# Column sums of a masked spectral kernel moved by two units and into the tail's norm, two gathers issued earlier, and a ring of 15 tiles instead of 13

## The chip, the cores and the metric

The kernel runs on one core of a Trainium2 chip. The core has five instruction streams: TensorE (PE, with its weight loads listed as PEld), VectorE (DVE), ScalarE (ACT), GpSimd (POOL) and SyncE (SP, here used to issue DMAs). Every stream takes its instructions in the order in which the program gives them and waits on semaphores for the others. Sixteen DMA engines move data between the device memory and the on-chip memory. The metric is the time of one execution in microseconds (us); lower is better.

## What is computed

The input `x` is one image of 512 x 512 positions with 64 channels (67 MB in float32). Two layers are applied, each to a group-normalised copy of its input, and each added to its input:

```python
x = x + _L0_conv_ref(_gn(x), mask, ...)   # masked triangle product with gates
x = x + _L1_conv_ref(_gn(x), w_real, w_imag)

# layer 0: xn = ln(x); left, right = masked, gated projections of xn
out = jnp.einsum('bkjd,bkid->bijd', left, right)
out = (_ln(out) @ out_w + out_b) * sigmoid(xn @ ogate_w + ogate_b)

# layer 1: the lowest 12 x 12 modes of a 2-D Fourier transform, mixed over channels
x_ft = jnp.fft.fft2(xc, axes=(-2, -1))[:, :, :12, :12]
out_ft = jnp.einsum('bcmn,comn->bomn', x_ft, w)
out = real(ifft2(out_ft padded with zeros))
```

The second layer needs three things of the first layer's whole result `x1`: the mean and variance of each of 32 groups of channels, the 12 x 12 modes, and `x1` itself, to which the inverse transform is added.

## The kernel before

The kernel looks at the mask on the chip. If at most 256 rows are kept by it, which is so here, it takes the path `compact`, where rows of the image are sorted so that the kept ones come first. The first stages (to about 812 us) make the triangle product, which lies in `places`, a buffer of 8 places of 4096 floats per partition, and put its layer-normed, projected result in `u_d` in device memory.

**The unit loop.** `x1` is then made in 32 units. A unit is a pair of 32 image columns (`jc`, 16 of them) and a half of the rows (`half`, two blocks of 128 rows). A unit `v` has 8 steps `n`; `s` counts steps over all, `k = v + 8`. `last` is unit 31. Each step's work is written down by hand in the order in which the engines shall take it: PE transposes data 13 steps ahead (`transpose`), multiplies for the gate of this step (`times`, tile `w_ps`) and for the centred values 12 steps ahead (`c_ps`); every fourth step it adds into the row transform (`transform`). DVE multiplies by the inverse deviation (L1144), adds a bias, sums squares and makes the statistics of the second norm from the unit before (L1051). ACT evacuates, squares and takes the sigmoid. POOL multiplies the gate in (`gated`, L1002) and adds into `x1` (`added`, L1006), and issues the gathers that load later units (`load`, L628). SP issues all stores of `x1` (`store`, into `x1_h[0]` for the left 256 image columns, `x1_h[1]` for the right), the 32 row loads of `u_d` for every second unit (`load_u`), and the writes of the row transform (`save`, into `modes_d`). In units `v % 4 == 1` the statistics of four units are joined (`join_means`, `join_squares`, `join_rest`).

**The column sums.** The column part of the transform is taken in four pieces of 128 image columns, `h` = 0 to 3. `fetch(h)` loads a piece of `modes_d` into `modes_t` (place 7, first part), and `columns(h, pool)` has PE do 12 small matmuls on it (24 passes in the trace, L888) into a PSUM tile of the transposes' pool `t_ps`, which has two slots, and DVE add them to `sums` (L889). In the loop the load is issued on SP in step 6 of units 8, 16 and 24 (L1167) and the sums come in step 6 of units 9, 17 and 25 (L1169):

```python
if n == 6 and v % 8 == 0 and 0 < v < len(units):
    fetch(v // 8 - 1)
if n == 6 and v % 8 == 1 and 8 < v < len(units):
    columns(v // 8 - 1, ps_t)
```

In unit 30, SP issues the load of the mixing weights `wide` into places 3 to 5 (L1173; float positions 12288 to 21504).

**The tail.** POOL clears `picks`, the mixing's operand (L1192), loads the fourth piece of modes (`fetch(3)`, on POOL), then issues `AHEAD` = 13 gathers, each of one tile of `x1` (128 rows x 32 image columns x 64 channels, 1,048,576 bytes) from `x1_h` into a ring of buffers: one behind `wide` in `places` (positions 21504 to 23552), halves of the places 6, 2, 0, 1 and 7, and three extra tiles `lx_t`. Meanwhile DVE and PE finish the second norm (`group_norm_affine`: a reduction, the matmul `mean_ps`, five DVE operations, the matmul `var_ps`, the inverse root), then do `columns(3)`, the product `turned`, the filling of `picks`, 288 small matmuls that mix the channels (`mixed_ps`, L1224), and the inverse transform over columns (`back_columns`). After that 64 tiles are finished one by one: four matmuls (`l_ps`, L1286), four additions on DVE (L1293), a store by SP (L1294), and a gather of the tile that is 13 further on into the same buffer (L1298 to L1300). Three more `back_columns` come between.

Of the kernel before, what the change touches and what calls it, by code (L numbers as in the profile page):

```python
# [17 lines left out]
P = 128  # L18
# [13 lines left out]
K = 2 * P  # L32
AHEAD = 13
SHARE = 22
# [12 lines left out]
def conv_preact_kernel(ctx: ExitStack, tc: tile.TileContext, t: dict):  # L47
# [135 lines left out]
    def rsqrt(pool, total, scale, eps, shape, y=None):  # L183

        out, steps = rsqrt_steps(pool, total, scale, eps, shape, y)
        for step in steps:
            step()
        return out  # L190
# [49 lines left out]

    def group_norm_affine(keep, sets, each, name):

# [4 lines left out]
        with tc.tile_pool(name="gn_" + name, bufs=1) as gp, tc.tile_pool(  # L247
# [4 lines left out]
            mean_ps = gps.tile([P, groups], F32, name="mean_ps")  # L252
            nc.tensor.matmul(mean_ps, avg, part, start=True, stop=True)
            mean = gp.tile([P, groups], F32, name="mean")
            nc.vector.tensor_scalar(mean, mean_ps, 1.0 / (n * each), None, ALU.mult)
# [8 lines left out]
            var_ps = gps.tile([P, groups], F32, name="var_ps")  # L264
            nc.tensor.matmul(var_ps, avg, v, start=True, stop=True)
            rs = rsqrt(gp, var_ps, 1.0 / n, EPS, [P, groups])
            if groups == G:
# [344 lines left out]
    def compact(fc):  # L612
# [193 lines left out]
        with tc.tile_pool(name="tri", bufs=1) as trp:  # L806
# [57 lines left out]
            with tc.manual_schedule(), tc.tile_pool(name="late", bufs=1) as lp:  # L864
# [17 lines left out]

                def columns(h, pool):
                    by = modes_t.rearrange("p (m k) c -> p m (k c)", k=2)
                    ps = pool.tile([P, 4, P], F32, name="t_ps").rearrange("p i k -> p (i k)")[:, : MODES * M2]
                    ps = ps.rearrange("p (m n) -> p m n", m=MODES)
                    for m in range(MODES):
                        nc.tensor.matmul(ps[:, m, :], by[:, m, :], col_basis[:, h, :], start=True, stop=True)  # L888
                    nc.vector.tensor_add(sums, sums, ps)  # L889

                def fetch(h):

                    (nc.gpsimd if h == 3 else nc.sync).dma_start(modes_t, modes_d[h * P : (h + 1) * P])

                with tc.tile_pool(name="np_x", bufs=LEAD + 2) as tp, tc.tile_pool(
# [179 lines left out]
                    for s in range(-LEAD, total_g + 2 * SIZE):  # L1075
# [44 lines left out]
                        if 0 <= v + 3 < len(units):  # L1120
                            if n == 3:
                                load(v + 3, 0)
                            if n == 6:
                                load(v + 3, 1)

                        if n >= 3 and held(1):
# [40 lines left out]
                        if n == 6 and v % 8 == 0 and 0 < v < len(units):  # L1167
                            fetch(v // 8 - 1)
                        if n == 6 and v % 8 == 1 and 8 < v < len(units):  # L1169
                            columns(v // 8 - 1, ps_t)  # L1170
# [4 lines left out]
                with tc.tile_pool(name="lq", bufs=1) as qp, tc.tile_pool(name="lx", bufs=1) as xp:  # L1175

                    free = 3 * 64 * C + C * MODES * MODES
                    buffers = [places[:, free : free + JC * C].rearrange("p (n c) -> p n c", c=C)]
                    buffers += [place(i)[:, r * JC : (r + 1) * JC] for i in (6, 2, 0, 1) for r in range(2)]
                    buffers += [place(7)[:, JC:]]  # L1180
                    buffers += [xp.tile([P, JC, C], F32, name=f"lx_t{i}") for i in range(AHEAD - len(buffers))]
                    ranked = [h.rearrange("s (k j) c -> (s k) (j c)", k=NJ // 2) for h in x1_h]
                    tiles_left = [(jc, b) for jc in range(NJ) for b in range(4)]
                    xts = {}

                    def fetch_rows(jc, b):
                        xts[jc, b] = buffers[(4 * jc + b) % AHEAD]
                        gather(xts[jc, b].rearrange("p j c -> p (j c)"), ranked[jc // 8], dst_i, b, jc % 8)


                    picks = qp.tile([P, MODES, MODES, 32], F32, name="picks")
                    nc.gpsimd.memset(picks, 0.0)  # L1192
                    fetch(3)
                    for jb in tiles_left[:AHEAD]:
                        fetch_rows(*jb)
                    rinv = qp.tile([P, 4, P], F32, name="rinv")
                    nc.scalar.dma_start(rinv, t["c_rinv"])
                    col_inv = qp.tile([P, 2, 4, P], F32, name="col_inv")
                    nc.scalar.dma_start(col_inv, t["c_col_inv"])
                    ab2 = group_norm_affine(lp, sets, 8, "x1c")  # L1200
                    with tc.tile_pool(name="tcp", bufs=1, space=PSUM) as tcp:
                        columns(3, tcp)
                    with tc.tile_pool(name="sps", bufs=1, space=PSUM) as sps:
# [16 lines left out]
                        for m3 in range(3):  # L1220
                            for n in range(MODES):
                                for g in range(4):
# [3 lines left out]
                                        start=(n == 0), stop=(n == MODES - 1), tile_position=(0, 32 * g),  # L1226
                                    )

                        mixed = qp.tile([P, 3, C], F32, name="mixed")
# [45 lines left out]
                    with tc.tile_pool(name="lpq", bufs=1, space=PSUM) as pq, tc.tile_pool(  # L1275
                        name="lpt", bufs=2, space=PSUM
                    ) as pt, tc.tile_pool(name="lps", bufs=4, space=PSUM) as pp:
                        for jc in range(NJ):
                            for b in range(4):
                                it = parts[:, jc // 8, (jc % 8) * N : (jc % 8 + 1) * N]  # L1280
                                xt = xts.pop((jc, b))
                                group = []
# [16 lines left out]
                                if ahead < len(tiles_left):  # L1299
                                    fetch_rows(*tiles_left[ahead])  # L1300
                                if jc % 4 == 1 and b == 0 and jc // 4 < 3:
# [72 lines left out]
```

## Time and profile before

| what | us |
|---|---|
| median of three runs (1876.83 to 1881.99) | 1879.58 |
| the profiled execution, its own time | 1877.87 |
| its span, first to last instruction | 1876.0 |
| unit loop, units 0 to 31 (812 to 1534.8) | 723 |
| end of the loop to the first finished tiles (1534.8 to 1580) | 45 |
| tiles of the second layer (1580 to 1876) | 296 |

The page gives, over the span, PE 88% busy, DVE 78%, ACT 51%, POOL 47%, and 250 GB/s moved by DMA on average. A span's mean hides that the stages differ, so the shares are to be read by stage: PE is busy for 674 of the 723 us of the unit loop, DVE for 675; the DMA engines are busy for 0.98 of the last 296 us. A line of the timeline reads: start, duration, engine, line of the program, operation, result and operands, count, and in brackets how long the engine had been idle before it and what ended that.

### The profile page before, as it was taken

Reading aid. Unit: us, or ns where it says so; the run is one execution under the profiler, and the core shown is the slowest. Engines: PE = TensorE matmul, PEld = TensorE weight load, DVE = VectorE, ACT = ScalarE, POOL = GpSimd, SP = SyncE. Lnnn points to the kernel's source line nnn. Section 1 sums busy time; section 2 is a strip of 40 time slices with the busy share of each in tenths; the row PEclk is TensorE's granted clock in tenths of the full one; section 3 lists DMA queues with packets and bytes.
Section 4 is the critical chain, followed back from the end, with each engine's and each line's share of the span. In section 5 each row is a group of like instructions: output and inputs, shape, how many; then the busy total and the mean of one; then the engine's idle time right before and its main releaser. Section 6 shows DMA issues by size and latency. Waiting matters only on the chain. (4 is left out here: it accounts for less than half of the span.)

```text
span 1876.0 us, 33850 instructions
## 1 busy us (share of the span) xinstructions
PE 1653.0 (88%) x11598; PEld 1302.6 (69%) x11598; DVE 1454.2 (78%) x3001; ACT 953.8 (51%) x1670; POOL 873.8 (47%) x678
## 2 busy tenths in 40 slices
PE   6779899999899999899998999899989957997873
PEld 5666666664787777788887988788879835664441
DVE  5989677777455559989998899899989994664552
ACT  3665466554222278777776677677757720111000
POOL 3655111111000000059999799989979982111110
PEclk9989899999899999999999999999989976555555
DMA  6999155556655534347876677767666599999999
GB/s 251 390 380 377 59 135 139 140 138 160 206 180 175 168 127 180 136 151 263 267 258 231 226 252 252 266 222 241 235 240 229 189 252 365 414 426 427 426 427 382
DMA packets 188869, 468.23 MB, mean 250 GB/s; under 512 B 35184, under 2 KB 134384, under 8 KB 147600
## 3 DMA queue, kind: packets, MB, share of 16 engines
q1 hardware_dynamic: 158192, 262.40, 41.3%
q0 software_dynamic: 27856, 202.19, 28.0%
q8 instruction: 94, 1.54, 0.3%
q10 hardware_dynamic: 2640, 1.38, 0.3%
q14 instruction: 87, 0.71, 0.1%
HBM read 278.13 MB, written 187.76 MB: 248 GB/s over the span
## 5 line engine op out<-in xcount | busy, mean ns | idle before, releaser
L943 PE MATMUL w_ps<-gate_x,xt_c 128*128 128x128 f32 x2048 | 283.3, 283 | 30.2 <-DVE z_t L1144 28.8
L1006 POOL TENSOR_TENSOR places<-places,z_t 128x1024 f32<-128x1024 f32 x127 | 301.8, 2377 | 8.2
L943 PEld LDWEIGHTS w_ps<-gate_x,xt_c 128*128 128x128 f32 x2048 | 254.4, 195 | 47.5 <-DVE z_t L1144 45.7
L943 PE MATMUL c_ps<-center_x,xt_c 128*128 128x128 f32 x2048 | 277.7, 279 | 6.1 <-ACT xt_c L938 5.5
L943 PEld LDWEIGHTS c_ps<-center_x,xt_c 128*128 128x128 f32 x2048 | 253.5, 195 | 9.9 <-ACT xt_c L938 7.8
L1286 PE MATMUL l_ps<-places,rinv 24*128 24x512 f32 x512 | 211.3, 1128 | 33.2 <-DVE places L1293 27.1
L1051 DVE BATCH_NORM_STATS2 stats2c<-places 128x6 f32<-128x128 f32 x1024 | 220.4, 278 | 8.2 <-POOL places L1006 8.2
L976 DVE TENSOR_REDUCE scratch<-sq_c 128x16 f32<-128x1024 f32 x160 | 194.6, 1216 | 21.7 <-ACT sq_c L971 7.6
L1100 ACT ACTIVATE z_t<-z_t 128x1024 f32<-128x1024 f32 x128 | 135.4, 1058 | 141.9 <-DVE z_t L1147 120.2
L1147 DVE TENSOR_TENSOR z_t<-z_t,scratch 128x1024 f32<-128x1024 f32 x160 | 195.4, 1221 | 11.3 <-ACT rs_n L982 3.3
L1286 PEld LDWEIGHTS l_ps<-places,rinv 24*128 24x128 f32 x512 | 120.9, 304 | 118.5 <-DVE places L1293 74.8
L933 PE MATMUL t_ps<-c_ident,places 128*128 128x128 f32 x1280 | 201.4, 281 | 1.3 <-DVE places L853 1.3
L1002 POOL TENSOR_TENSOR z_t<-z_t,bias_row_out 128x1024 f32<-128x1024 f32 x63 | 149.7, 2376 | 101.2 <-ACT z_t L1100 101.0
L1293 DVE TENSOR_TENSOR places<-places,l_ps 128x512 f32<-128x512 f32 x200 | 124.0, 682 | 89.8 <-DMA places<-x_h,dst_i 58.3
L938 ACT ACTIVATE xt_c<-t_ps,ab_xc 128x512 f32<-128x512 f32 x256 | 176.1, 688 | 34.4 <-PE t_ps L933 27.7
L933 PEld LDWEIGHTS t_ps<-c_ident,places 128*128 128x128 f32 x1280 | 146.6, 143 | 59.6 <-issue 50.4
L628 POOL DMA_INDIRECT places<-in_x,src_i x64 | 62.6, 978 | 258.0 <-PE t_ps L933 247.3
L1144 DVE TENSOR_TENSOR z_t<-w_ps,rs_n 128x512 f32<-128x512 f32 x256 | 171.9, 672 | 7.4 <-PE w_ps L943 7.4
L1002 POOL TENSOR_TENSOR z_t<-z_t,places 128x1024 f32<-128x1024 f32 x64 | 151.5, 2367 | 35.9 <-ACT z_t L1100 35.7
L968 ACT ACTIVATE sq_c<-c_ps 128x512 f32<-128x512 f32 x256 | 150.7, 589 | 31.4 <-PE c_ps L943 31.1
L678 DVE BATCH_NORM_STATS2 stats1c<-x_ps 128x6 f32<-128x512 f32 x256 | 155.3, 680 | 13.4 <-PE x_ps L677 13.4
L663 ACT COPY xc<-xg 128x128 f32 x352 | 105.0, 298 | 67.5 <-POOL xc L663 43.5
(206 smaller groups left out, 2607.5 us busy)
## 6 DMA issues: line engine op xcount, KB each, us to landing
x_h<-places SPq DMA_DIRECT2D x64, 1024.0 KB
out_x<-places SPq DMA_DIRECT2D x50, 1024.0 KB
places<-u_d SPq DMA_DIRECT2D x512, 64.0 KB
left_d<-o_c SPq DMA_DIRECT2D x64, 256.0 KB
right_d<-o_c SPq DMA_DIRECT2D x64, 256.0 KB
left_raw<-left_d SPq DMA_DIRECT2D x64, 256.0 KB
right_raw<-right_d SPq DMA_DIRECT2D x64, 256.0 KB
u_d<-z_t SPq DMA_DIRECT2D x32, 512.0 KB
```

The source lines that it names most:

```text
L678: nc.vector.bn_stats(stats[:, 0, 16 * (jc % quarter) + 4 * r + c, :], ps.rearrange("p i k -> p (i k)"))
L933: nc.tensor.transpose(tps[:, i, :], flat[:, o : o + P], ident)
L938: nc.scalar.activation(xts[s], tps, AF.Identity, bias=ab1[:, 2:3])
L943: nc.tensor.matmul(ps[:, 2 * i : 2 * i + 2, :], xts[s][:, i, :], w, start=True, stop=True)
L968: nc.scalar.activation(sq, cps, AF.Square)
L976: nc.vector.tensor_reduce(totals[k % 2][:, 8 * (n - 1) : 8 * (n + 1)], sqs.pop(s // 2), AX.X, ALU.add)
L1002: nc.gpsimd.tensor_mul(zs[k, c], zs[k, c], u)
L1006: nc.gpsimd.tensor_add(xr, xr, zs.pop((k, c)))
L1051: nc.vector.bn_stats(st[k // 4][:, g, k % 4, :], x_of(k)[:, :, 2 * g : 2 * g + 2])
L1144: nc.vector.tensor_mul(z[:, 8 * odd : 8 * odd + 8, :], wps, rs)
L1147: nc.vector.tensor_add(z, z, bias.unsqueeze(1).to_broadcast([P, 16, C]))
L1286: nc.tensor.matmul(ps.rearrange("p j o -> p (j o)"), rinv[h, b, :], it[h], start=True, stop=True, tile_position=(32 * g, 0),)
```

## The change

- In the loop the column sums come in step 6 of units 11, 19 and 27. The loads stay where they are.
- `columns` is split: `column_sums` returns a list of 12 matmuls and the addition; `columns` runs through it. In the tail, `group_norm_affine` calls a function after each of its two matmuls, and the tail has it issue the matmuls 0 to 6 after `mean_ps` and 7 to 11 after `var_ps`; the addition follows the norm.
- `fetch_rows` and most of the ring's buffers are defined ahead of the loop. The gathers of tiles 0 and 1 are issued in step 3 of units 30 and 31, on POOL, after the loads' place in the step.
- `AHEAD` is 15. Two buffers of the ring, the last, lie in the memory of `picks`; their first gathers are issued after the mixing matmuls. Before those, tiles 2 to 12 are gathered as before.

```diff
-AHEAD = 13
+AHEAD = 15
...
-    def group_norm_affine(keep, sets, each, name):
+    def group_norm_affine(keep, sets, each, name, between=lambda i: None):
...
             nc.tensor.matmul(mean_ps, avg, part, start=True, stop=True)
+            between(0)
...
             nc.tensor.matmul(var_ps, avg, v, start=True, stop=True)
+            between(1)
...
-                def columns(h, pool):
+                def column_sums(h, pool):
+
                     by = modes_t.rearrange("p (m k) c -> p m (k c)", k=2)
...
-                    for m in range(MODES):
-                        nc.tensor.matmul(ps[:, m, :], by[:, m, :], col_basis[:, h, :], start=True, stop=True)
-                    nc.vector.tensor_add(sums, sums, ps)
+                    steps = [
+                        lambda m=m: nc.tensor.matmul(ps[:, m, :], by[:, m, :], col_basis[:, h, :], start=True, stop=True)
+                        for m in range(MODES)
+                    ]
+                    return steps + [lambda: nc.vector.tensor_add(sums, sums, ps)]
+
+                def columns(h, pool):
+                    for step in column_sums(h, pool):
+                        step()
...
+                free = 3 * 64 * C + C * MODES * MODES
+                buffers = [places[:, free : free + JC * C].rearrange("p (n c) -> p n c", c=C)]
+                buffers += [place(i)[:, r * JC : (r + 1) * JC] for i in (6, 2, 0, 1) for r in range(2)]
+                buffers += [place(7)[:, JC:]]
+                ranked = [h.rearrange("s (k j) c -> (s k) (j c)", k=NJ // 2) for h in x1_h]
+                tiles_left = [(jc, b) for jc in range(NJ) for b in range(4)]
+                fetched = {}
+
+                def fetch_rows(i):
+                    jc, b = tiles_left[i]
+                    fetched[jc, b] = buffers[i % AHEAD]
+                    gather(fetched[jc, b].rearrange("p j c -> p (j c)"), ranked[jc // 8], dst_i, b, jc % 8)
...
+                        if (v, n) in ((last - 1, 3), (last, 3)):
+                            fetch_rows(len(fetched))
...
-                        if n == 6 and v % 8 == 1 and 8 < v < len(units):
+                        if n == 6 and v % 8 == 3 and 8 < v < len(units):
                             columns(v // 8 - 1, ps_t)
...
-                    for jb in tiles_left[:AHEAD]:
-                        fetch_rows(*jb)
+                    buffers += [xp.tile([P, JC, C], F32, name=f"lx_t{i}") for i in range(AHEAD - 2 - len(buffers))]
+                    spare = picks.rearrange("p m n k -> p (m n k)")
+                    buffers += [spare[:, i * JC * C : (i + 1) * JC * C].rearrange("p (n c) -> p n c", c=C) for i in range(2)]
+                    for i in range(len(fetched), AHEAD - 2):
+                        fetch_rows(i)
...
-                    ab2 = group_norm_affine(lp, sets, 8, "x1c")
                     with tc.tile_pool(name="tcp", bufs=1, space=PSUM) as tcp:
-                        columns(3, tcp)
+                        steps = column_sums(3, tcp)
+
+                        def some(i):
+                            for step in steps[7 * i : 7 * i + 7 - 2 * i]:
+                                step()
+
+                        ab2 = group_norm_affine(lp, sets, 8, "x1c", some)
+                        steps[-1]()
...
+                        for i in range(AHEAD - 2, AHEAD):
+                            fetch_rows(i)
...
-                                    fetch_rows(*tiles_left[ahead])
+                                    fetch_rows(ahead)
```

More of the change, by code (lines that the diff above doesn't have):

```diff
@@ L1175, in compact @@
                 with tc.tile_pool(name="lq", bufs=1) as qp, tc.tile_pool(name="lx", bufs=1) as xp:
[L1177 to L1188, printed above, removed]
                     picks = qp.tile([P, MODES, MODES, 32], F32, name="picks")
@@ L1280, in compact @@
                                 it = parts[:, jc // 8, (jc % 8) * N : (jc % 8 + 1) * N]
-                                xt = xts.pop((jc, b))
+                                xt = fetched.pop((jc, b))
                                 group = []
```

## The prediction

> **What bounds the kernel now.** I read the page's forty slices first (46.9 us each): from slice 16 on VectorE (DVE) is full, in the last seven slices the DMA engines are.
>
> ```profile
> DVE  5989677777455559989998899899989994664552
> DMA  6999155556655534347876677767666599999999
> ```
>
> So there are two stages to price: the unit loop (812 to 1534 us) and the tail behind it. To cut the loop into units I took the one reciprocal that each unit issues on DVE (L1138; in the timeline at 983.85, 1004.83, 1036.93, 1060.31 us and so on), and asked for the busy time of each engine between them. Columns: stretch, us, busy us of PE, PEld, DVE, ACT, POOL, TensorE clock, DMA share, GB/s.
>
> ```profile
> 983.90:1004.80 20.90, 20.63 (x178) 18.22 (x177) 20.69 (x50) 16.02 (x25) 20.35 (x11) 1.00 0.70 265
> 1004.80:1036.90 32.10, 24.28 (x180) 21.57 (x180) 23.61 (x56) 16.48 (x26) 26.01 (x13) 0.87 0.72 246
> 1036.90:1060.30 23.40, 23.40 (x198) 21.48 (x198) 21.04 (x50) 16.70 (x25) 16.61 (x9) 0.95 0.48 171
> 1102.30:1126.40 24.10, 21.78 (x176) 19.46 (x175) 23.13 (x56) 16.60 (x26) 21.89 (x12) 0.93 0.77 249
> 1189.30:1217.60 28.30, 23.34 (x180) 20.62 (x179) 23.68 (x57) 16.52 (x26) 26.11 (x13) 0.92 0.79 275
> 1217.60:1241.10 23.50, 23.50 (x198) 21.58 (x198) 21.02 (x51) 16.67 (x25) 16.66 (x9) 0.95 0.50 173
> 1369.90:1400.80 30.90, 24.27 (x180) 21.55 (x179) 23.60 (x57) 16.46 (x26) 26.02 (x13) 0.89 0.75 252
> 1400.80:1424.80 24.00, 24.00 (x198) 22.08 (x198) 20.98 (x50) 16.74 (x25) 16.57 (x9) 0.93 0.48 170
> ```
>
> A plain unit (first line, v = 8) takes 20.97 us from reciprocal to reciprocal, and DVE is busy for 20.7 of them: DVE sets the pace, PE and POOL are close behind. A unit with the joining of statistics (v = 13, fourth line) takes 24.1. The units with column sums (v = 9, 17, 25) also join, and take 32.1, 28.3 and 30.9; each is followed by one of 23.4 to 24.0 where 20.97 is plain. The timeline around the first shows why:
>
> ```profile
> 1024.71 0.35 SPq L893 DMA_DIRECT2D places<-modes_d  x1
> 1030.45 5.29 PE L888 MATMUL t_ps<-col_basis,places 128*128 128x24 f32 x24 [5.71 <-DMA places<-modes_d]
> 1035.78 0.45 DVE L889 TENSOR_TENSOR sums<-sums,t_ps 128x288 f32<-128x288 f32 x1 [7.94 <-PE t_ps L888]
> 1036.46 1.91 PE L943 MATMUL w_ps<-gate_x,xt_c 128*128 128x128 f32 x8
> ```
>
> The load of the modes was written 21 us of program earlier, but SP reaches it at 1024.7, behind its stores and the 32 row loads of a unit. It lands 5.7 us later, PE stands before the column matmuls, DVE behind them for 7.9. The other two sums show the same, with 2.8 and 4.5 us on PE (13.0 for the three by the waits of L888) and 4.1 and 6.8 on DVE.
>
> In the tail I read the chain of waits in order of time, then the DMA engines.
>
> ```profile
> 1549.87 6.40 PE t_ps L888 x24
> 1556.28 0.47 DVE sums L889
> 1556.79 1.33 PE turned L1206 x2
> 1532.50:1542.50 10.00, 2.06 (x8) 0.33 (x8) 10.00 (x44) 0.59 (x1) 7.15 (x4) 0.58 0.54 191
> 1547.50:1580.00 32.50, 21.39 (x352) 18.75 (x352) 10.33 (x34) 3.68 (x4) 8.33 (x9) 0.73 1.01 415
> 1580.00:1587.50 7.50, 6.74 (x24) 4.20 (x24) 5.68 (x10) 0.00 (x0) 0.00 (x0) 0.62 0.46 190
> 1620.00:1850.00 230.00, 192.21 (x492) 112.80 (x488) 131.07 (x212) 13.38 (x16) 42.19 (x45) 0.50 1.01 426
> ```
>
> The last column sums stand wholly on the chain, after the norm's second matmul. The DMA engines are full at 426 GB/s from 1547 to the end but for a hole near 1582: the 13 gathers have landed and no tile has been stored yet (first store issued at 1583.6). Before 1547 there is another hole, 1532 to 1547. One 1,048,576-byte tile costs 2.46 us at 426 GB/s, so in this stage time is won only by closing holes.
>
> **The Trainium skill.** "Perfetto Trace Analysis", Sequencer Loop: an engine's sequencer takes its instructions in order, each waiting for its semaphores. The trace agrees: nothing of PE runs in the 5.71 us, though the transposes behind L888 need none of that load. "TensorE: Matmul & The Clock Gate", Part 1, has the array fall to half clock after an idle window of some 3.4 us and return after as long a busy one. The trace agrees: after the stall the 24 column matmuls take 5.29 us, and the next eight (w_ps) 1.91 instead of 1.06. After the shorter stall of 2.8 us the columns took 4.30, so the threshold isn't seen that sharply. "DMA: Bandwidth & Descriptors", Queues, rings and completion order, says that each DMA engine goes round its queues packet by packet; I use it for the gathers beside other transfers, which the tail before shows only as gathers and stores sharing half and half.
>
> **The change part by part.**
>
> *Column sums two units later.* What they cost: 32.1 + 23.4 - 24.0 - 20.97 = 10.5 us; 28.3 + 23.5 - 45.0 = 6.8; 30.9 + 24.0 - 45.0 = 10.0; together 27.3 (24.0 is a joining unit, between 23.9 and 24.1). Now the load, issued at 1024.7, has some 40 us, and the wait goes. What is late next? PE's lead decides. In v = 11 the matmuls of step 6 end at 1077.7, and DVE frees itself from the product of that step at 1080.6 (0.68 from 1079.90). Eight weight loads of the same size take 0.97 at full clock, so 24 take 2.9: the columns end at 1080.6, just as DVE arrives. Left are the addition on DVE, 0.45, and PE catching up: its step without waits takes 2.23 (1077.69 less 1075.47) against 2.62 of DVE's, so the lead comes back in eight steps. I take 1.5 us for each sum; at best 0.5 (the addition alone), at worst 5 (columns uncovered or at half clock). The PSUM slot that the sums take from the transposes is asked for again two steps later, 2 us after the addition. The load itself stays put. Gain 27.3 - 4.5 = 22.8; bounds 12.3 and 25.8.
>
> *Two gathers in the last units.* On POOL each costs 0.98 us and some 0.15 of issue, queued before the gate products of units 30 and 31. The buffers (the upper part of places 5, and half of 6) were last read by POOL's own products one or two steps before, so they should not wait. The first is swallowed by POOL's 1.7 us idle at 1509; from 1511 on POOL has no gap, and its last addition (1532.45 to 1534.8) releases the last statistics: the second costs 1.2 us on the chain. On the DMA side both ride beside the mixing weights (1500 to 1525, queue full) and push weights and stores back by 2 x 2.46 = 4.9 us, into the hole of 1532 to 1542, which has 4.6 us free. The small writes of the last modes (issued 1537.6) then meet x stores that before were nearly over, and the load of the modes, issued at 1541.2, comes at about 1544.3: 1.2 from POOL and an estimated 1.9 of queueing. The other 11 gathers start 3.0 later. Net on DMA: 4.9 - 3.0 = 1.9 us ahead. If the modes are hardly held up, 3.7; if they are held 4 us more, -2.
>
> *Columns between the norm's matmuls.* In the tail 24 matmuls take 5.32 us. Fourteen now stand before var_ps, ten behind it. The modes land at about 1548.5, columns until 1551.6, var_ps (0.65) until 1552.3; then DVE's 15 small operations (2.95 us, 1549.62 to 1552.57 before) beside the ten (2.2), until 1555.3; addition, turned, picks as before, so mixing starts at 1558.7 instead of 1559.7: 1.0 us earlier. Bounds: 2.8 (all else on time) and -3.
>
> *Two more buffers.* Tiles 13 and 14 go into the picks' memory once the mixing matmuls are read out of it (1569). The hole is 7.5 x (1 - 0.46) = 4.0 us; by stretches of 2.5 us the gathers end at about 1580.7 and the stores' data begin at 1584.4. Thirteen tiles now end at 1580.7 - 1.9 = 1578.8; two more keep the queue full until 1583.7, while the stores' data begin at 1583.4. The hole closes. From there the loop is as before: a tile takes 2.85 us on DVE against 4.9 of DMA, and the pause of the stores at 1594 to 1605 stays. Gain 4.0, bounds 0 and 6.
>
> The tail together: 1.9 + 4.0 is 5.9, say 6.1 with the small places around 1607 where DMA falls below 1.0. The earlier mixing isn't added: it is within the closing of the hole.
>
> Sum: 22.8 + 6.1 = 28.9. The profiled execution took 1877.87 (span 1876.0): 1849.0. The median of the runs lies 1.7 above it; I forecast 1850.
>
> **Rivals.**
> A. The columns keep most of their cost: PE's lead isn't there when they come. For it: PE is busy 20.6 of 20.9 us in plain units, and there is no joining in v = 11 that lets it run ahead. Against: 2.9 us between PE's and DVE's step 6. At 5 us each: 1877.9 - 12.3 - 6.1 = 1859.5.
> B. The tail gives nothing: the gathers hold up the last modes as long as they save, mixing starts 3 to 4 us later, and the hole is only moved. For it: small packets beside large ones. 1877.9 - 22.8 = 1855.
> C. Slower: POOL stands at the first gather in unit 30 (1500 us) because its wait takes in a transfer to the neighbouring part of places, the weights, which land by 1525 and later with company. All gate products of the last two units queue behind it, DVE's statistics and PE's transform behind those. It decides from 29 us on; POOL held until 1531 would make it 1877.9 - 22.8 - 4 + 31 = 1882. Against: the weights are issued after it, and the buffer begins where they end.
> D. The change doesn't do what it says: the sums meet another wait in their new place, 9 us each. 1877 to 1879. Nothing in v = 11, 19, 27 speaks for it.
>
> **How the numbers follow.** Likeliest 0.66, A 0.13, B 0.15, C 0.04, D 0.02. Range: both the best ends (25.8 and 9) give 1843, a little under for the median's spread: 1842; upward it takes in A and B: 1862. A measurement of this kernel can't tell less than about 0.3% (5.6 us) from no change. Faster: the first three, 0.94; within 0.3%: D, 0.02; slower: C, 0.04.
>
> **What would show it.** Each step in the new trace: L888 waits for no DMA in the loop, its 24 matmuls take about 3 us, DVE idles under 1 us before L889; the units 9, 17, 25 take 24 us and those after 20.97; POOL's two gathers have no idle time before them; the start of mixed_ps lies 1 us earlier against the end of the last statistics' wait; no hole in DMA between 1575 and 1590 of the old count. It is wrong if a wait of PE or DVE of over 3 us stands in units 11, 19 or 27, if the modes of the tail land more than 4 us later, or if DMA falls under 400 GB/s in a new place before the first store.

## The result and the profile after

The kernel after takes 1854.95 us (median of four runs, 1853.24 to 1856.55), beside 1878.2 us of the kernel before on the same chip (1875.72 to 1881.99). The ratio is 0.9875, interval 0.9856 to 0.9894: 23 us faster. The profiled execution took 1856.55 with a span of 1854.8, which is 21.2 less than the span of before. The prediction said 28.9 less. Line numbers below are those of the kernel profiled: in the one after, the column matmuls stand at L891, the addition to `sums` at L894, the loads of the modes at L902, the gathers at L630, the stores of finished tiles at L1317.

The page's slices for the kernel after (DVE busy, DMA busy, in tenths) show a shorter loop, and, among the last eight slices (from 1484 us on), an 8 in the second (1530 to 1577 us), where the first tiles are finished:

```profile
DVE  5989677777455559999999999999999984665552
DMA  6999255556655525347767776687676598999998
```

**The loop.** I cut it at the reciprocals again (L1164). The same columns as in the prediction: stretch, us, busy us of PE, PEld, DVE, ACT, POOL, clock, DMA share, GB/s. The rows are units 8, 9, 11, 12, 20 and 28 of the kernel after.

```profile
983.60:1004.50 20.90, 20.64 (x178) 18.23 (x177) 20.69 (x50) 16.01 (x25) 20.35 (x11) 1.00 0.70 265
1004.50:1028.30 23.80, 21.19 (x179) 18.40 (x179) 23.25 (x56) 16.58 (x26) 22.19 (x12) 1.00 0.64 186
1049.20:1070.70 21.50, 21.38 (x181) 19.07 (x181) 21.28 (x52) 16.17 (x24) 20.95 (x11) 0.98 0.76 250
1070.70:1094.00 23.30, 23.30 (x197) 21.38 (x196) 20.97 (x50) 16.32 (x25) 20.94 (x11) 0.95 0.69 253
1247.40:1269.10 21.70, 21.70 (x193) 19.78 (x192) 20.84 (x51) 16.25 (x24) 20.38 (x10) 1.00 0.69 257
1422.00:1445.40 23.40, 23.40 (x196) 21.48 (x196) 21.07 (x51) 16.27 (x25) 21.07 (x11) 0.94 0.67 247
```

Unit 9 is now a plain joining unit, with 23.8 instead of 32.1. The sums sit in unit 11, which takes 21.5 where 20.97 is plain. What the prediction had not seen stands in the column of the clock: units 12 and 28 have 0.95 and 0.94 and last 23.3 and 23.4, while unit 20 kept its clock at 1.00 and lasts 21.7. The timeline around the first sums shows where the clock was lost:

```profile
1064.94 1.06 PE L967 MATMUL w_ps<-gate_x,xt_c 128*128 128x128 f32 x8
1066.72 2.76 PE L891 MATMUL t_ps<-col_basis,places 128*128 128x24 f32 x24
1069.52 0.45 DVE L894 TENSOR_TENSOR sums<-sums,t_ps 128x288 f32<-128x288 f32 x1
1069.89 1.91 PE L967 MATMUL w_ps<-gate_x,xt_c 128*128 128x128 f32 x8
1071.85 0.69 DVE L1170 TENSOR_TENSOR z_t<-w_ps,rs_n 128x512 f32<-128x512 f32 x1 [0.64 <-PE w_ps L967]
```

No wait stands before L891, its 24 passes take 2.76, and DVE comes to the addition without idle time. But the next eight gate passes take 1.91 instead of 1.06, without any stall ahead of them.

**The tail.** The timeline of the kernel after, from the second early gather on (cut to the steps of the argument):

```profile
1501.62 0.98 POOL L630 DMA_INDIRECT places<-x_h,dst_i  x1 [0.15 <-issue]
1514.44 3.94 POOL L1204 MEMSET picks<- 128x4608 f32 x1
1517.27 1.99 ACTq L1069 DMA_DIRECT2D modes_d<-places  x4
1522.92 0.37 ACTq L1212 DMA_DIRECT2D rinv<-in_c_rinv  x1
1523.33 0.44 ACTq L1214 DMA_DIRECT2D col_inv<-in_c_col_inv  x1
1524.13 0.59 POOL L902 DMA_DIRECT2D places<-modes_d  x1 [5.76 <-DMA modes_d<-places]
1530.48 3.18 PE L891 MATMUL t_ps<-col_basis,places 128*128 128x24 f32 x14 [5.02 <-DMA places<-modes_d]
1534.14 0.19 DVE L199 TENSOR_SCALAR rq_v<-var_ps 128x32 f32<-128x32 f32 x1 [6.62 <-PE var_ps L266]
1539.25 0.45 DVE L894 TENSOR_TENSOR sums<-sums,t_ps 128x288 f32<-128x288 f32 x1 [2.23 <-remote]
1566.32 3.19 SPq L1317 DMA_DIRECT2D out_x<-places  x2
```

POOL comes to the gather without a wait. It then stands 5.76 us before the load of the modes, because the writes of the last modes (issued at 1517.27) have not landed. In the meantime ACT has issued the loads of two constants of the inverse transform, `rinv` and `col_inv` (256 and 512 KB), which in the kernel before come after the load of the modes. PE stands 5.02 before the first fourteen column passes, the norm's second matmul `var_ps` stands behind those, and DVE idles 6.62 and then, before the addition, 2.23 more. The chain of waits of the kernel after has the same stretch on its path:

```profile
1518.74 4.96 DMA modes_d<-places
...
1524.13 6.30 DMA places<-modes_d
...
1530.48 3.18 PE t_ps L891 x14
1533.66 0.46 PE var_ps L266 x2
...
1536.72 3.04 issue
```

To lay executions side by side I count the tail from the clearing of `picks` (the POOL memset: 1534.7 before, 1514.4 after). The hole in the DMA engines lies 45 to 60 us after it. In the windows of the kernel before, the first ten us and those fifteen:

```profile
1534.70:1544.70 10.00, 2.06 (x8) 0.33 (x8) 9.46 (x44) 0.99 (x2) 6.54 (x6) 0.50 0.60 198
...
1579.70:1594.70 15.00, 13.64 (x48) 9.40 (x48) 12.14 (x20) 0.45 (x2) 1.87 (x2) 0.57 0.70 257
```

And of the kernel after:

```profile
1514.40:1524.40 10.00, 1.94 (x8) 0.20 (x8) 9.15 (x42) 1.23 (x3) 4.24 (x3) 0.50 0.84 331
...
1559.40:1574.40 15.00, 13.14 (x48) 9.25 (x47) 11.45 (x18) 2.05 (x2) 1.50 (x2) 0.61 0.63 232
```

The early gathers did fill the first hole (331 GB/s for 198), and the second got deeper (232 for 257), in spite of two more buffers. From the reciprocal that ends unit 30 to the end of the span it is 365.5 us before and 365.6 after: the tail gave nothing. The gain is the loop's: from the reciprocal of unit 8 to that end, 526.7 us before and 505.6 after, 21.1.

### The profile page after: what moved, and what is told of

It is laid out like the page before. It is cut to its first block, busy times and chain, and to the rows that moved or that the text cites. A ratio compares the mean times of both kernels' runs of the same rounds, so it can differ in the third digit from the quotient of the medians.

```text
span 1854.8 us, 33850 instructions
## 1 busy us (share of the span) xinstructions
PE 1644.3 (89%) x11598; PEld 1295.3 (70%) x11598; DVE 1455.1 (78%) x3001; ACT 952.9 (51%) x1670; POOL 873.7 (47%) x678
## 4 chain that ended last, share of the span: by engine, by line
PE 23%; DVE 22%; DMA 8%; POOL 5%; issue 3%; ACT 2%; SPq 1%; DVEq 0%; ACTq 0%; POOLq 0%
DVE scratch L1000 5%; DVE z_t L1170 5%; DVE z_t L1173 5%; PE w_ps L967 5%; PE l_ps L1309 5%; PE c_ps L967 5%; DVE stats2c L1075 4%; DMA places<-x_h,dst_i 4%; POOL z_t L1026 3%; PE t_ps L957 3%; DMA out_x<-places 2%; PE f_ps L1057 2%; POOL places L1030 2%; PE y_ps L978 1%; DMA picks<-x_h,dst_i 1%
## 5 line engine op out<-in xcount | busy, mean ns | idle before, releaser
L1309 PE MATMUL l_ps<-places,rinv 24*128 24x512 f32 x512 | 206.7, 1128 | 29.2 <-DVE places L1316 18.0
L1000 DVE TENSOR_REDUCE scratch<-sq_c 128x16 f32<-128x1024 f32 x160 | 194.5, 1216 | 21.7 <-ACT sq_c L995 7.6
L630 POOL DMA_INDIRECT places<-in_x,src_i x64 | 62.6, 978 | 258.5 <-PE t_ps L957 246.9
L1316 DVE TENSOR_TENSOR places<-places,l_ps 128x512 f32<-128x512 f32 x176 | 109.3, 682 | 79.3 <-PE l_ps L1309 39.8
```

The source lines that it names most:

```text
L1000: nc.vector.tensor_reduce(totals[k % 2][:, 8 * (n - 1) : 8 * (n + 1)], sqs.pop(s // 2), AX.X, ALU.add)
L1309: nc.tensor.matmul(ps.rearrange("p j o -> p (j o)"), rinv[h, b, :], it[h], start=True, stop=True, tile_position=(32 * g, 0),)
```

## The experiments

A table first, of each profiled execution, in us after the clearing of `picks`: when the load of the fourth piece of modes is issued, when its column matmuls start, the addition to `sums`, the first store, the end; then the GB/s of the 15 us of the hole, and the loop as above. The kernels with a gather in unit 31 (after, e3_spread, e8_order) clear 1.1 us later against the loop.

```text
kernel          load  columns  addition  store    end   GB/s   loop
before           6.5    15.1     21.6     48.9   341.3   257   526.7
after            9.7    16.0     24.8     51.9   340.3   232   505.6
e1_sums          6.5    15.1     20.5     48.6   339.9   259   504.1
e2_late          6.5    11.9     18.6     45.8   333.7   424   505.6
e3_spread       10.3    15.6     22.2     50.2   336.5   273   502.3
e4_late_spread   6.5    11.9     18.4     45.9   333.1   425   501.9
e5_ring13        6.5    11.9     21.5     49.0   340.3   246   502.2
e6_nonorm        6.5    14.7     21.6     50.0   337.7   382   501.8
e7_gap           6.5    13.2     20.2     47.8   335.3   345   502.1
e8_order         6.4    11.8     18.2     51.3   339.2   281   501.8
e9_first         8.4    12.8     19.4     47.1   334.8   406   502.1
e10_norm         6.5    11.9     18.6     45.3   336.9   348   530.2
```

Spans themselves are not compared: the loop starts up to 8 us earlier or later from one execution to another (978 to 986), with the same program ahead of it. Two executions of an unchanged tail (before and e1_sums) differ by 1.4 in it, and of an unchanged loop (before and e10_norm) by 3.5; differences under that are not read from one profile.

**The sums alone.** The kernel before with one number changed:

```diff
-if n == 6 and v % 8 == 1 and 8 < v < len(units):
+if n == 6 and v % 8 == 3 and 8 < v < len(units):
```

> The kernel before with the column sums moved to units 11, 19 and 27, nothing else. Theory (all of the gain is the loop's, the three changes of the tail cancel each other): the loop ends 21.4 us earlier as in the changed kernel, the tail takes the 341 us of before, time 0.988 of before (about 1856). Rival (the tail changes still gain the 6 us forecast, and the loop gave less): time about 1861, loop only 15 us shorter.

Measured: 1848.67 us, ratio 0.9872 (0.9849 to 0.9896); the loop takes 504.1, the tail 339.9, the hole keeps its 259 GB/s. This one number has the whole gain of the change, as the theory said. In this execution one of the three sums was followed by half clock, against two of three in the one after.

**Without the early gathers.** The kernel after less two lines:

```diff
-if (v, n) in ((last - 1, 3), (last, 3)):
-    fetch_rows(len(fetched))
```

> The changed kernel without the two gathers in units 30 and 31; tiles 0 to 12 are gathered in the tail. Theory (the two gathers push the last stores of x1 back by 5 us, the last writes of the modes wait behind those stores): the load of the modes is issued 4 us earlier against the end of the loop, PE waits under 1 us for it instead of 5.0, mixing starts 2 to 3 us earlier than in before against the loop's end, the hole in DMA of 5 us before the first stores is gone, time about 1850 to 1851. Rival (the gathers save what they cost, the hole has another cause): time 1855 to 1857.

Measured: 1846.19 us, ratio 0.9851 (0.9833 to 0.9869). The modes are loaded 6.5 us after the clearing, the columns start without a wait, the hole is gone (424 GB/s), and the tail is 6.6 shorter than after's, besides the 1.1 of the clearing. The loop is that of the kernel after (505.6 in both). The times alone do not show it: the interval overlaps with that of the kernel after.

**The sums in groups.** The kernel after with the twelve matmuls of a sum (24 passes) in three groups of four, with other matmuls of step 6 between them:

```diff
+    steps = column_sums(v // 8 - 1, ps_t)
+for step in steps[:4]:
+    step()
     wps = raw(s) if k < first else times(ps_w, "w_ps", s, gate_x)
+for step in steps[4:8]:
+    step()
...
-    columns(v // 8 - 1, ps_t)
+for step in steps[8:]:
+    step()
```

> The changed kernel with the 12 column matmuls of step 6 issued in three groups of 4: after the transposes, after the gate product, after the centred values. Theory (24 thin passes in a row make TensorE's clock fall to half for some 3 us, and units 12 and 28 pay 2.4 us for it): those units take 21.0 to 21.5 instead of 23.35, clock 1.00, time 4 to 5 us less, about 1850. Rival (the 2.4 us are PE getting its lead back after 2.8 us of extra work, whatever the clock): units 12 and 28 stay at 23, time as the changed kernel, 1855.

Measured: 1847.71 us, ratio 0.9868 (0.9851 to 0.9886). Each group of eight passes takes 0.97, and the gate passes after the last keep 1.06, as the timeline of e3_spread shows:

```profile
1063.18 0.97 PE L891 MATMUL t_ps<-col_basis,places 128*128 128x24 f32 x8
1064.97 0.97 PE L891 MATMUL t_ps<-col_basis,places 128*128 128x24 f32 x8
1066.75 0.97 PE L891 MATMUL t_ps<-col_basis,places 128*128 128x24 f32 x8
1068.04 1.06 PE L967 MATMUL w_ps<-gate_x,xt_c 128*128 128x128 f32 x8
```

Its unit 12, in the windows, has a clock of 1.00 and 21.7 us instead of 23.3:

```profile
1068.90:1090.60 21.70, 21.70 (x193) 19.78 (x192) 20.85 (x50) 16.22 (x25) 20.91 (x11) 1.00 0.69 263
```

The loop takes 502.3, 3.3 less than after's. Over the profiled executions of the kernels with sums in one run (after, e1_sums, e2_late), half clock followed 5 of 9 sums; of the seven with groups, 0 of 21.

Which sums pay can be read from the trace's own record of the granted clock. In the kernel after, the 18 changes of clock between 700 and 1500 us all lie on one grid of 3.413 us, to within 0.001 us. The nine sums in one run, with the longest part of each that lies in one interval of its execution's grid:

```text
kernel    unit   sum             longest part   half clock from
after      11    1066.72-1069.48     2.76         1069.68
           19    1243.41-1246.16     2.40         none
           27    1418.10-1420.86     2.76         1421.25
e1_sums    11    1062.00-1064.76     1.57         none
           19    1237.05-1239.81     2.54         none
           27    1411.73-1414.48     2.76         1414.76
e2_late    11    1065.16-1067.92     2.76         1067.95
           19    1241.83-1244.59     2.56         none
           27    1416.55-1419.31     2.76         1419.52
```

The reader is to see that the five sums that lie wholly in one interval are the five that are followed by half clock, from the end of that interval on and for one interval. The four that an interval's edge cuts are not. A sum in groups has at most 1.94 us of its passes in one interval.

A sum costs some 1.2 us where the clock stays (0.47 in its unit, 0.75 in the next), and 2.9 where it falls. In the run's time the 3 us cannot be seen: the interval overlaps with that of the kernel after.

**Both together.** Groups, and no early gathers:

> Both of the last two edits: no gathers in units 30 and 31, and the column matmuls in three groups. If both theories hold, the gains add: 1846. If only the gathers matter 1850, if only the clock matters 1850, if neither 1855.

Measured: 1841.77 us, ratio 0.9832 (0.9814 to 0.985). It is faster than both kernels; the interval does not meet that of the kernel after. Multiplied by the 1878.2 us of before on the chip of the kernel after, the ratio gives 1846.6, which is the 1846 expected if both theories hold. On the same chip the five runs of e3_spread (1846.59 to 1851.89) all lie above the five of e4_late_spread (1839.39 to 1845.79), so the harm of the early gathers is in the times too. Its tail in the timeline:

```profile
1514.67 0.59 POOL L902 DMA_DIRECT2D places<-modes_d  x1 [2.52 <-DMA modes_d<-places]
1520.12 3.16 PE L891 MATMUL t_ps<-col_basis,places 128*128 128x24 f32 x14
1523.76 0.19 DVE L199 TENSOR_SCALAR rq_v<-var_ps 128x32 f32<-128x32 f32 x1 [1.33 <-PE var_ps L266]
1526.61 0.44 DVE L894 TENSOR_TENSOR sums<-sums,t_ps 128x288 f32<-128x288 f32 x1
```

PE has no wait before the columns, DVE 1.33 where after had 6.62, and none before the addition. The hole is closed, by its windows:

```profile
1553.20:1568.20 15.00, 13.31 (x48) 9.49 (x46) 10.83 (x18) 1.49 (x3) 1.68 (x2) 0.50 1.01 425
```

**One gather instead of two.** e3_spread with the early gather of unit 30 alone, a test by dose:

```diff
-if (v, n) in ((last - 1, 3), (last, 3)):
+if (v, n) == (last - 1, 3):
```

> The kernel after with the grouped sums of e3_spread, and of the two early gathers only the one in unit 30. Theory (the gathers push the last x stores back by what they carry, and the writes of the last modes stand behind those stores): one gather pushes back by 2.5 us instead of 4.9, so the load of the modes is issued at about 8.4 us after the clearing of picks (6.5 without early gathers, 10.3 with two); the tail from the clearing takes some 335 us, between 333.1 and 336.5; the time lies at the middle of e4_late_spread and e3_spread, some 3 us under e3_spread beside the same kernel before. Rival (what costs is the work of POOL in unit 31 or the second gather's place in its queue, not the bytes): the load of the modes is back at 6.5 and the tail at 333. Second rival (any early gather costs the whole): 10 and 336.5.

Measured: 1844.48 us, ratio 0.9827 (0.9798 to 0.9857). The load of the modes is issued at 8.4, and the end comes at 334.8, as the theory of displaced stores had it; both rivals gave other numbers. The time of the load tells them apart (6.5 and 10 by the rivals); the end alone would not, at 1.8 from one rival and 1.7 from the other, where an unchanged tail varied by 1.4. From the reciprocal that ends unit 30 to the end of the span none, one and two early gathers (e4_late_spread, e9_first, e3_spread) take 357.3, 359.0 and 361.7. In the time of the runs one gather costs nothing that can be told from none.

Why the modes come late I read from the packets in the trace: the share of the 16 DMA engines that SP's queue (stores of `x1`) and ACT's queue (writes of the last modes) took in each us after the clearing. The writes are issued at 2.8 to 2.9 in all three.

```text
us after the clearing     2     3     4     5     6     7     8     9
before    SP stores    1.01  0.71  0.00  0.00  0.00  0.00  0.00  0.00
          ACT writes   0.00  0.21  0.50  0.57  0.00  0.00  0.00  0.00
e9_first  SP stores    1.01  1.01  1.01  0.71  0.06  0.00  0.00  0.00
          ACT writes   0.00  0.00  0.00  0.19  0.66  0.05  0.00  0.00
after     SP stores    1.01  1.01  1.01  1.01  0.94  0.29  0.01  0.00
          ACT writes   0.00  0.00  0.00  0.00  0.03  0.64  0.23  0.00
```

The reader is to see that the two rows hardly overlap. While the stores take 1.0 of the engines the writes do not move at all; in the kernel after their first packet comes 3.6 us after the issue. Whether the descriptors or the packets are held back, the trace does not say.

The load of the modes meets the same a second time. ACT issues the two constants 8.5 and 8.9 us after the clearing in the kernel after, and the load comes at 9.7. From 10 to 12 us the constants take 1.02 and 0.98 of the engines; the load has its first packet at 11.8 and its last at 15.7, 6.0 us after its issue. In before the load (6.5) is ahead of the constants (9.6 and 10.0) and its packets run from 7.8 to 10.6, 4.1 after the issue; there the constants wait, until 13.7, and then share the engines with the gathers. In e9_first the load (8.4) is still ahead of them (9.6) and is in by 12.5; in e3_spread it is behind them again (8.5 and 10.3) and is in by 15.3. So with none, one and two early gathers the modes are in 10.5, 12.5 and 15.3 us after the clearing (e4_late_spread, e9_first, e3_spread), and with the second the constants go first. No run here moved the constants alone, so what they cost by themselves is read from the packets only.

**The norm's interleaving alone**, on the kernel before (ring 13, no early gathers, sums in units 9, 17, 25):

> The kernel before with one part of the change alone: the last column matmuls 7 and 5 between the norm's two matmuls. Sums stay in units 9, 17, 25, the ring stays at 13 tiles, no early gathers. Theory (the interleaving alone is worth 3 us where the modes land in time): the columns start 11.9 us after the clearing of picks instead of 15.1, the first store is issued at about 46 instead of 48.9, the hole in the DMA engines before it shrinks from 6.0 us of full rate to about 3, and the tail takes 338 to 339 instead of 341.3; the unit loop stays at 526 to 527 us; time some 3 us under before, too little for the verdict. Rival (DVE, not PE, holds the mixing up, as the addition stood 3 us late in the ring of 13): columns at 11.9, the addition still at 21.5, first store at 49, tail 341: no change.

Measured: 1872.83 us, ratio 0.9984 (0.9971 to 0.9997), which is 3 us. The columns start at 11.9, the addition comes at 18.6, the first store at 45.3, the tail ends at 336.9. The theory holds, with a larger effect in the profile (4.4) than it named; but the tail of before has PE's signal to the addition 1.1 us late (see the end), and beside e1_sums, which has the same tail without that, the effect is 3.0. The loop was 3.5 longer than in the profile of before, with the same program: unit 17, with its wait for the modes, took 31.5 in place of 28.3.

**Without the interleaving**, e4_late_spread with `ab2 = group_norm_affine(lp, sets, 8, "x1c")` and then `columns(3, tcp)`:

> The fourth run with the last column sums again after the norm as in before, ring of 15 tiles kept. Theory (15 tiles cover until 51 us after the clearing, and the first store at 48.9 comes within that): no hole, tail 333 to 334, as in the fourth run; moving the matmuls between the norm's is then worth nothing beside the larger ring. Rival (the earlier store matters by itself): tail 336 to 337.

Measured: 1847.64 us, ratio 0.9834 (0.9809 to 0.9859). The columns start at 14.7 and the tail ends at 337.7, 4.6 later than in e4_late_spread: the rival holds, the earlier store matters by itself. In e6_nonorm too PE's signal came 1.6 late. So interleaving is worth between 3.0 and 4.6 in the profiles, where the modes land in time. Against its own runs of before this kernel is no slower than e4_late_spread is against its; the 4.6 us are not seen there, across two chips.

**Without the two buffers**, e4_late_spread with a ring of 13 and none in `picks`:

```diff
-AHEAD = 15
+AHEAD = 13
...
-for i in range(AHEAD - 2, AHEAD):
-    fetch_rows(i)
```

> The fourth run (no gathers in the last units, column matmuls in three groups) with the ring back at 13 tiles, none in the picks' memory. From the clearing of the picks to the end the fourth run took 333.1 us, before 341.3. Theory (both the earlier first store and the two more tiles are needed to close the hole of 4 us): the first store still comes at 45.8 us after the clearing instead of 48.9, but 13 tiles are in by 46, so 1 to 2 us of hole stay and the tail takes 335 to 336. Rival (the two tiles do it all): 338 to 339, hole of 4 us.

Measured: 1850.08 us, ratio 0.9843 (0.9817 to 0.9869), the tail 340.3. This pair gives 7.2 for the buffers, but it is spoiled: DVE stood 3 us before the addition, as in the kernel after, which e4_late_spread had not. The timeline of e5_ring13:

```profile
1528.10 2.31 PE L891 MATMUL t_ps<-col_basis,places 128*128 128x24 f32 x10
1534.31 0.45 DVE L894 TENSOR_TENSOR sums<-sums,t_ps 128x288 f32<-128x288 f32 x1 [3.04 <-remote]
```

The last column pass ends at 1530.4 by its record, and PE's signal arrives 3.9 us later; in the kernel after 3.0 later, while in e10_norm (also 13 tiles) DVE did not wait for it. So a ring of 13 does not bring it about by itself. The better pair is e10_norm and e4_late_spread, 13 and 15 tiles with no other difference in the program of the tail: 336.9 and 333.1, so 3.8 for the two buffers, from one profile of each. The hole of e10_norm is half open, by its windows:

```profile
1577.60:1592.60 15.00, 12.70 (x47) 8.98 (x44) 10.59 (x17) 2.09 (x4) 2.81 (x3) 0.50 0.93 348
```

**Two attempts to keep the early bytes without their harm.** In e7_gap, e4_late_spread has one gather, of tile 0, between the clearing of `picks` and the load of the modes, where the engines are idle:

> The fourth run with the gather of tile 0 issued right after the clearing of the picks, ahead of the load of the last modes. In that stretch DMA is idle for 4.6 us. Theory (a tile moved into idle time is worth its 2.46 us, if the modes come no later than PE reaches them, of which there is some 0.4 us): tail 331 to 332, modes 1 to 2 us later, mixing up to 1.5 later, no hole. Rival (it only holds up the modes, as the two gathers of the changed kernel do): tail 333 to 335.

Measured: 1848.38 us, ratio 0.9837 (0.9812 to 0.9862), no better than without. The first ten us move 280 GB/s for 198, but the load lands later (columns at 13.2, PE waits 1.1), the last gathers wait for earlier ones, and the tail ends 2.2 later than e4_late_spread's, where the rival had it. In e8_order, e3_spread has the writes of the last modes on SP's queue, in front of the last stores:

```diff
-queue = nc.scalar if jc == NJ - 1 else nc.sync
-queue.dma_start(modes_d[o : o + 8].rearrange("j m c -> m j c"), ft[32 * g : 32 * g + M2])
+nc.sync.dma_start(modes_d[o : o + 8].rearrange("j m c -> m j c"), ft[32 * g : 32 * g + M2])
```

> The changed kernel with the column matmuls in three groups (tail 336.5 us, load of the modes 10.3 us after the clearing), the gathers in units 30 and 31 kept, and the last four writes of the modes issued by SP ahead of the last two stores of x1 instead of by ACT beside them. Theory (the writes wait behind stores that were issued before them, and these are late because of the two gathers): the load of the modes is issued at 6 to 7 us after the clearing, PE waits under 2 us for it, tail 331 to 333. Rival (the writes are slow for another reason, their small packets for one): load at 10 us as before, tail 336.

Measured: 1849.91 us, ratio 0.9839 (0.9814 to 0.9863). The load is back at 6.4 and the addition at 18.2, the earliest of all, and yet the first store comes at 51.3. The timeline of e8_order:

```profile
1530.79 5.07 PE L1251 MATMUL mixed_ps<-places,picks 128*32 128x64 f32 x170 [1.57 <-issue]
1537.75 0.94 POOL L630 DMA_INDIRECT places<-x_h,dst_i  x1 [13.90 <-DMA x_h<-places]
1539.82 0.42 PE L1251 MATMUL mixed_ps<-places,picks 128*32 128x64 f32 x6 [0.34 <-issue]
1546.39 0.53 DVE L1260 COPY mixed<-mixed_ps 128x64 f32<-128x64 f32 x3 [15.71 <-PE mixed_ps L1251]
```

By the profile the gather waits 13.9 us on POOL for a store of `x1`, with all later gathers behind it. The last of these stores, now behind the writes, is issued only at 1526.3 (17 us after the clearing; in e3_spread 1.7 after it), and its packets run until 1536.6. What SP waited for after the writes, which were in by 1514.6, is not shown. The mixing matmuls, which need none of that, then come in fits of about five, with gaps that no wait in the profile explains, and DVE idles 15.71 instead of the 10.32 of e3_spread. The writes came in time and another wait took the place of theirs.

## Why the prediction was nearly right in time and wrong in the tail

**The column sums: right, with one term too small.** The stall is gone and the joining units are plain, as the prediction had it. Its "I take 1.5 us for each sum" should have been 2.9, 1.2 and 2.9; 0.3 less in each joining unit gives some of it back, so that 21.1 of 22.8 came. The step that failed is that "24 take 2.9" at full clock and then nothing: they take 2.76, but the run costs the clock afterwards. Half clock stood only in its "at worst 5", for the columns themselves. The prediction had read in the Trainium skill, "TensorE: Matmul & The Clock Gate", Part 1, of a fall after an idle window; here it fell after 2.76 us of matmuls 24 columns wide, back to back, in 5 sums of 9. The same part says that the window is 3413 ns long and runs freely of the program. The trace agrees: the changes of clock lie on a grid of 3.413 us, and where on it a sum fell went in all nine with whether it paid. With groups the term is 1.2 and the loop gains 24.4 to 24.9, above the prediction.

**The early gathers: the sign was wrong.** The prediction's parts on POOL hold: no wait, and the clearing 1.1 us later (1.2 said). It failed in "the load of the modes ... comes at about 1544.3: 1.2 from POOL and an estimated 1.9 of queueing", and in "the modes land at about 1548.5". Against the loop the load was issued 4.3 us later in place of 3.1, and the columns then started 6.3 us after it in place of 4.2: the modes were there 3.3 us later than the prediction had them. Two terms were wrong. The 1.9 of queueing for the writes measured 3.2 (load 9.7 after the clearing for 6.5). And the load itself, for which the prediction kept the 4.2 of before, found the two constants ahead of it, which the prediction had not priced: 2.1 us more. Its own sign of being wrong, "if the modes of the tail land more than 4 us later", came: the last packet of the load is 6.1 us later against the loop. Behind the 1.9 was a round robin packet by packet, from the Trainium skill, "DMA: Bandwidth & Descriptors", Queues, rings and completion order. The trace does not show it between these two queues: in each us with SP's stores at 1.0 of the engines ACT's writes moved nothing. It does not refute it either: the page gives a packet some 9 to 17 descriptors, and a store has 128 rows of 8 KB for 16 engines, so by an estimate from these one packet may take in an engine's whole share of a store. The "if they are held 4 us more, -2" named among the ends was the case that came: two gathers cost 4.4 us (e4_late_spread to e3_spread) where 1.9 were to be gained.

**The norm: larger than said, and undone by the gathers.** With the modes in time it brings 3.0 to 4.6 where the prediction said 1.0 and did not add it; 2.8 was its bound for "all else on time". In the kernel after it works the other way round: `var_ps` stands behind columns that stand behind the load, so that DVE waits 6.62 for a matmul that needs no modes. The prediction had this only in its bound of -3.

**The two buffers: right where the mixing is on time.** 3.8 for the 4.0 said. In the kernel after the mixing starts 4.3 us later against the loop, the gathers of tiles 13 and 14 go out at 1553.5, 39 us after the clearing (32 in e4_late_spread), the first store comes later too, and the hole stays. The sign that the prediction named, "no hole in DMA between 1575 and 1590 of the old count", is the one that failed.

**The sum.** Without early gathers the tail gains 8.2 (before to e4_late_spread), of which 4.4 and 3.8 are the norm and the buffers, each to within the 1.4 by which an unchanged tail varied. The gathers take 4.4 of that back (e3_spread). The kernel after lacks another 3.9 beside e3_spread, with the same program in the tail. In part that is the late signal before the addition (24.8 for 22.2), but the first store is only 1.7 later; the rest stays open. So of the cases that were priced rival B, "the gathers hold up the last modes as long as they save, mixing starts 3 to 4 us later, and the hole is only moved", came nearest to what took place, with its 1855. It had 0.15, and the likeliest case 0.66. That the tail came to nothing so exactly is chance: it is 8.2 less 4.4 less 3.9, and the last has no cause in the program that was found.

## What to carry to other kernels

A transfer that is moved earlier displaces what rode there; ask which small transfer on another queue will now stand behind the displaced bytes, and who waits for it. Do not put work that waits for a load ahead of work that needs none on the same engine, unless the load is early by more than its worst delay. And a run of thin matmuls was better dealt out among wide ones than issued in one piece. Look as well at transfers that nobody waits for yet: here 768 KB of constants, issued 0.8 us ahead of an urgent load, went ahead of it, and the load took 6.0 us to land for 4.1.

## What was not expected of the hardware

- TensorE at half clock after 2.76 us of thin passes with no idle time ahead: the next eight gate passes took 1.91 us for 1.06. It came whenever the whole 2.76 us lay in one interval of the clock's 3.413 us grid (5 of 5), and not when at most 2.56 did (0 of 4). In groups of eight passes it did not happen in 21 sums.
- Small writes on ACT's queue did not move while 1 MB stores on SP's queue filled the engines: first packet 3.6 us after the issue, 0.8 where the stores were ending. The load of the modes on POOL's queue did not move while the constants on ACT's queue did so: first packet 2.1 us after the issue for 1.3 in before.
- PE's signal for the last column pass reached DVE 3.0 us after the recorded end of the pass in the kernel after, 3.9 in e5_ring13, 1.6 in e6_nonorm, 1.1 in before, and at once in e1_sums. Recorded ends of matmuls are modelled, so the pass itself may have been late. Its cause stays open, and with it how much of the 3.9 above would be there in another execution. The same holds for the gaps between the mixing matmuls in e8_order.
